# A two-layer graph transformer on one core: VectorE's order, the neighbour lists and their gathers around the first block

## The chip, the cores and the metric

The kernel runs on one NeuronCore of a Trainium2 chip. Its engines are TensorE (PE), VectorE (DVE), ScalarE (ACT), GpSimd (POOL) and SyncE (SP); each takes its instructions in the order of its own queue, and they wait for each other through semaphores. The metric is the device time of one execution in microseconds. Differences under 0.2% count as none here.

## The reference

`x` is 2708 x 512, `adj` a sparse symmetric 0/1 matrix of 2708 x 2708 with a set diagonal. Two layers of the same form are applied:

```
mask   = adj + I
q,k,v  = h @ Wq.T + bq, h @ Wk.T + bk, h @ Wv.T + bv      (8 heads of 64)
scores = q k^T / 8, and -1e9 where mask == 0
ctx    = softmax(scores) v
h1     = layer_norm(h + ctx @ Wo.T + bo)
h2     = layer_norm(h1 + relu(h1 @ W1.T + b1) @ W2.T + b2)     (2048 wide)
```

A token has few neighbours (at most 22 or so), so each row's softmax needs only those columns.

## The kernel before

**By edges.** `by_edges` makes for each token a list of its neighbours (`LIST` = 24 places) and gathers only their rows of keys and values. Tokens are ranked by the length of their list and placed anew in 22 tiles of 128, so that all tokens of a tile have nearly equal lists; `CAPS` has the length per tile. If a check on list lengths or scores fails (`flags`), a second path, `by_rows`, does the whole work densely behind a branch (`tc.If(again > 0)`).

**First pass** (`first`). For 22 tiles of tokens TensorE makes keys and values; ScalarE's queue stores them to `kv_d[0]`. Beside it the rows of `adj` are loaded, and VectorE takes each row's largest codes (`lists`). `counted` and `ranked` sort the tokens by counting; `rec` holds for each token its neighbours' numbers plus one (0: none), 32 words to a token, and goes to `rec_d`. `inverted` multiplies one-hot tables (`one`, `who`) on TensorE to get `ident_i`, the token at each new place.

**Second pass** (`first_queries`). For 22 tiles, `t` = 0 to 21, TensorE makes the queries `q` from `xT` (loads `xg` by SP), VectorE adds the bias (`qs`, L959), SP stores to `q_d`. At `t == 4` come `inverted` and the first gathers by GpSimd: 22 gathers `new<-rec_d` in all (`fetched`), some at once and later two per tile, one for each place tile. `listed` turns parts of `new` into `idx` (what the gathers of keys go by) and `minus` (what the exponential adds), at `t` = 6, 17 and 21. `new` is allotted with the tag of `hT`, the transposed input of the feed-forward, of which there is one buffer.

**Attention** (`attend`, class `Tile`). For each place tile in the order 20, 19, 18, 17, 7, 9, 6, ... the list is cut in chunks of two neighbours (the last may be one). I number the chunks: tile 20 has c1 to c3, tile 19 c4 to c6, tile 18 c7 to c10, tile 17 c11 to c14, tile 7 c15 to c19, tile 9 c20 to c24; c3, c10 and c14 have one neighbour. A chunk is: gathers `kv<-kv_d` by GpSimd, one per neighbour (five buffers, later a sixth); VectorE `kv<-kv,q` and the reduction `sc` (the scores); ScalarE `p` (exponential) and half of the weighting; VectorE `kv<-kv,p` and `acc`. A tile ends with `su`, its reciprocal, and ScalarE's division into `cx`. Gathers are asked for three chunks ahead.

**Blocks.** Two place tiles are a block: (20, 19), (18, 17), (7, 9), ... `attended` transposes `cx` (TensorE `tp`, ScalarE `cT`), multiplies by Wo (`o`) and norms (`h`, with `rd` made by GpSimd). `turned` transposes `h` into `hT`. `feed_forward` does 16 steps f: `pf` (TensorE), `ft` (ScalarE), and, three steps behind, `a`. Between the steps `advance` sends some attention for the blocks to come; at f = 10 or 11 the next block's `attended` begins.

**Who sets the order.** TensorE, ScalarE and SP follow the program's order throughout. GpSimd follows it in the first two passes and in block 0. VectorE follows it in the second pass; elsewhere a scheduler places its instructions, and it may place one of block 0 among those of the second pass.

Of the kernel before, what the change touches and what calls it, by code (L numbers as in the profile page):

```python
# [18 lines left out]
P = 128  # L19
DM = 512  # L20
# [32 lines left out]
def by_rows(ctx: ExitStack, tc: tile.TileContext, x, xT, adj, layers, out):  # L53
# [33 lines left out]
    def project(w, srcT):  # L87
# [3 lines left out]
        with tc.tile_pool(name="pw", bufs=1) as pw, tc.tile_pool(  # L91
# [20 lines left out]
            for i, (b, bw) in enumerate(blocks):  # L112
# [17 lines left out]
                for m in range(NC):  # L130
# [27 lines left out]
    def attend(kT, v):  # L158

        with tc.tile_pool(name="aq", bufs=2) as aq, tc.tile_pool(  # L160
# [130 lines left out]
            def finish(t, j, s, rb, ct):  # L291
                weigh(t, j, s, rb, ct)
                if j == NP - 1:
                    q0, r = t * P, min(P, N - t * P)
                    nc.gpsimd.dma_start(out=chunked(cT_d)[:, :, q0 : q0 + r], in_=ct[:, :, :r])

# [13 lines left out]
    def feed_forward(w, src, dst, dstT):  # L310
# [3 lines left out]
        with tc.tile_pool(name="fw", bufs=1) as fw, tc.tile_pool(  # L314
# [110 lines left out]
            def finish(i, hs, fts):  # L425
                b, bw = blocks[i]
                oT = None
                if dstT is not None:
                    oT = fx.tile([P, NC, TB], F32, tag="cg", name="oT")
                for n, t0 in enumerate(range(0, bw, P)):  # L430
                    r = min(P, bw - t0)
                    ps = ps_o.tile([P, DM], F32, tag="po", name="po")
                    for f in range(NFC):
                        nc.tensor.matmul(
                            ps[:r],
                            fts[f][:, t0 : t0 + r],
                            w2[:, f, :],
                            start=(f == 0),
                            stop=(f == NFC - 1),
                        )  # L440
# [3 lines left out]
                    nc.gpsimd.dma_start(out=dst[b + t0 : b + t0 + r, :], in_=z[:r])  # L444
                    if oT is not None:
                        flip(z, r, oT, t0)
                if oT is not None:
                    nc.gpsimd.dma_start(out=chunked(dstT)[:, :, b : b + bw], in_=oT[:, :, :bw])

# [22 lines left out]
def by_edges(ctx: ExitStack, tc: tile.TileContext, x, xT, adj, layers, out, good):  # L472
# [130 lines left out]
    def lists_of(pa):  # L603
# [21 lines left out]
        nc.gpsimd.memset(top[:, NT - 1, :], 0.0)  # L625
        rec = pa.tile([P, NT, 32], F32, tag="rec", name="rec", bufs=1)
        nc.gpsimd.memset(rec, 0.0)

# [10 lines left out]

        token = counting("token", [P, NT], [[P, NT]], 1)  # L640
        starts = counting("starts", [P, NT], [[P, NT]], 0)
# [18 lines left out]
        )  # L660
        new = dn.tile([P, NC, 2 * P], F32, tag="hT", name="new", bufs=1)
        new = new.rearrange("p c t -> p (c t)")[:, : NT * 32]
        new = new.rearrange("p (g c) -> p g c", c=32)
        nc.gpsimd.memset(new[:, NT - 1, :], 0.0)

        full = []
# [34 lines left out]
        def counted():  # L701
# [52 lines left out]
            nc.vector.tensor_scalar(flags[:, 0:1], most, 0.5, None, ALU.is_le)  # L754
            nc.vector.tensor_tensor(rec[:, :, :LIST], has, low, ALU.mult)
            return hot, before, half

        def ranked(hot, before, half):
# [39 lines left out]
            for h in range(2):  # L798
                ts = slice(h * half, (h + 1) * half)
                table = pa.tile([P, N], F32, tag=f"code{h}", name="table", bufs=1)  # L800
                wide = half * P
                one = table[:, :wide].rearrange("p (t c) -> p t c", c=P)
                who = table[:, wide : wide + half * NT].rearrange("p (t g) -> p t g", g=NT)
# [15 lines left out]
                parts.append((one, who))  # L819
            return parts  # L820

        def inverted(parts):
# [3 lines left out]
            for one, who in parts:  # L826
                for i in range(NT // 2):
                    r = size(t)
                    nc.tensor.matmul(
                        to[:, :NT],  # L830
                        one[:r, i, :],
                        who[:r, i, :],
                        start=(t == 0),
                        stop=(t == NT - 1),
                    )
                    t += 1
            nc.vector.tensor_copy(ident_i, to[:, :NT])

        def fetched(tiles):

            for g in tiles:
                r = size(g)
                gather(new[:r, g, :], rec_d, ident_i[:r, g : g + 1])

        def listed(a, b):

            some = new[:, a:b, :LIST]
            nc.vector.tensor_scalar(idx[:, a:b, :], some, 1.0, 1.0, ALU.max, ALU.subtract)
            nc.vector.tensor_scalar(minus[:, a:b, :], some, 0.0, NEG, ALU.is_equal, ALU.mult)

        return lists, counted, (ranked, inverted, fetched, listed)

# [75 lines left out]
    def first_queries(bq, wq, counts, placing, pa, tokens, meanwhile):  # L928

        nonlocal at  # L930
        ranked, inverted, fetched, listed = placing
        later = [g for g in order[4:] if 5 <= g < 12] + [g for g in order[4:] if not 5 <= g < 12]
        made = []
# [11 lines left out]
        for t in range(NT):  # L945
# [16 lines left out]
            plus_rest(qs[:r, t % 2], q, r, DK**-0.5)  # L962
            if t == OWN - 1:
                listed(NT - 5, NT - 1)
                pa.__exit__(None, None, None)
                at = ctx.enter_context(tc.tile_pool(name="at", bufs=2))
                for g in order[:3]:
                    own[g] = at.tile([P, DM], F32, tag="q", name="q", bufs=QB)
                to = dict(own)
                next(ahead)  # L970
            if t == OWN:
# [4 lines left out]
            if t == OWN + 1:  # L976
                xr = own_rows(order[3])
            if OWN < t and later:
                fetched(later[:2])
                del later[:2]  # L980
            if t == NT - 5:
                listed(5, 12)
            if t == NT - 1:
                for a, b in ((0, 5), (12, NT - 5), (NT - 1, NT)):
                    listed(a, b)
# [12 lines left out]
    def own_rows(g):  # L998
# [579 lines left out]
    def beside_queries(t):  # L1578
# [19 lines left out]

    with tc.manual_schedule(engines={mybir.EngineType.Pool}):
        made = first(layers[0], beside_keys)  # L1600
        with tc.manual_schedule(engines={mybir.EngineType.DVE}):
            first_queries(*made, beside_queries)
    behind, pool = None, []
    for n in range(NL):
# [26 lines left out]
        turning = projecting = None  # L1631
        in_order = ExitStack()
        if n == 0:
            in_order.enter_context(tc.manual_schedule(engines={mybir.EngineType.Pool}))
        for k, block in enumerate(blocks):
# [136 lines left out]
```

## Time and profile before

| | us |
|---|---|
| median of 3 runs | 1958.9 (1958.81 to 1961.58) |
| the profiled execution, whole | 1959.88 |
| its span | 1958.1 |
| TensorE busy | 1866.8 (95%) |
| VectorE busy | 1327.6 (68%) |
| ScalarE busy | 931.8 (48%) |
| GpSimd busy | 806.0 (41%) |

A line of a timeline has the start, the duration, the engine, the line of the code, the operation, what is written and read, and how often; in brackets is the engine's idle time before it and what it is taken to have waited for. A line of waits has the total, the number and the longest. "PEclk" is the granted TensorE clock in tenths.

### The profile page before, as it was taken

The page shows a single profiled execution, that of the slowest core. Times are in us where ns is not written, and L with a number is a line of the kernel's source. Part 1 is how long each engine was busy: PE and PEld are TensorE (multiplying, and loading weights), DVE is VectorE, ACT ScalarE, POOL GpSimd, SP SyncE. Part 2 cuts the span into 40 slices and gives each one's busy share as a digit, 9 for nine tenths or more (in the row PEclk, how much of TensorE's full clock was granted, in tenths as well). Part 3 has the DMA queues.
Part 4 walks back from the last instruction along what each step waited for, and adds up shares of the span by engine and source line. Part 5 has one row for each costly group of instructions (what it writes and reads, how often), then busy time and mean ns, then how long its engine had stood idle before and what let it go on. Part 6 is the DMA issues. An engine that isn't in the chain of part 4 may idle for free.

```text
span 1958.1 us, 20966 instructions
## 1 busy us (share of the span) xinstructions
PE 1866.8 (95%) x6206; PEld 1104.6 (56%) x6206; DVE 1327.6 (68%) x2188; ACT 931.8 (48%) x3219; POOL 806.0 (41%) x705
## 2 busy tenths in 40 slices
PE   9999958999999999999999997999999999999996
PEld 4444425656566566655665553566566665666663
DVE  6886665768659686685840237786977998877421
ACT  4560324645546655564451113565475767654410
POOL 2112724445536555363410124444554775545110
PEclk9999978999999999999999998999999999999998
DMA  8999837455545656454401468556665766643000
GB/s 326 356 303 321 286 112 262 167 190 194 193 144 198 212 181 209 162 184 159 148 17 65 135 242 335 179 208 205 201 220 160 255 221 220 207 155 121 17 8 11
DMA packets 133915, 366.57 MB, mean 187 GB/s; under 512 B 19290, under 2 KB 39594, under 8 KB 131084
## 3 DMA queue, kind: packets, MB, share of 16 engines
q0 software_dynamic: 68816, 245.66, 38.0%
q1 hardware_dynamic: 53332, 99.66, 14.6%
q10 hardware_dynamic: 11644, 19.83, 2.8%
q8 instruction: 50, 0.82, 0.2%
q14 instruction: 73, 0.60, 0.1%
HBM read 314.62 MB, written 50.48 MB: 186 GB/s over the span
## 4 chain that ended last, share of the span: by engine, by line
PE 40%; DVE 8%; issue 5%; DMA 3%; POOL 2%; ACT 1%; SPq 0%; POOLq 0%; DVEq 0%
PE pf L1420 16%; PE a L1393 16%; PE o L575 4%; DMA kv<-kv_d,idx 2%; DVE kv L1092 2%; DVE sc L1098 1%; PE k L575 1%; PE v L575 1%; PE tp L1228 1%; POOL kv L1055 1%; DVE acc L1131 1%; DVE kv L1124 1%; DMA q<-q_d 1%; POOL rd L1218 1%; PE q L575 1%
## 5 line engine op out<-in xcount | busy, mean ns | idle before, releaser
L1055 POOL DMA_INDIRECT kv<-kv_d,idx x420 | 548.3, 1305 | 444.1 <-DVE acc L1131 271.0
L1420 PE MATMUL pf<-hT,w 128*128 128x256 f32 (+1 forms) x2816 | 637.7, 374 | 24.0 <-ACT hT L1233 14.4
L1420 PEld LDWEIGHTS pf<-hT,w 128*128 128x128 f32 x2816 | 521.3, 191 | 198.6 <-issue 103.9
L1393 PE MATMUL a<-w,ft 128*128 128x512 f32 x1312 | 619.8, 599 | 10.4 <-ACT ft L1431 7.8
L1092 DVE TENSOR_TENSOR kv<-kv,q 128x1024 f32<-128x1024 f32 (+3 forms) x222 | 254.0, 1155 | 206.8 <-DMA kv<-kv_d,idx 175.3
L1393 PEld LDWEIGHTS a<-w,ft 128*128 128x128 f32 x1312 | 249.5, 192 | 204.8 <-issue 170.5
L1431 ACT ACTIVATE ft<-pf,b 128x256 f32<-128x256 f32 (+1 forms) x336 | 154.1, 464 | 436.9 <-PE pf L1420 436.6
L1118 ACT ACTIVATE kv<-kv,p 128x64 f32<-128x64 f32 x1232 | 311.0, 335 | 5.0
L1098 DVE TENSOR_REDUCE sc<-kv 128x16 f32<-128x1024 f32 (+3 forms) x222 | 253.7, 1151 | 1.8
L1131 DVE TENSOR_TENSOR acc<-acc,kv 128x1024 f32<-128x1024 f32 (+2 forms) x178 | 203.7, 1144 | 19.8 <-ACT kv L1118 17.3
L1218 POOL TENSOR_TENSOR rd<-va,mhalf 128x1 f32<-128x1 f32 (+1 forms) x88 | 90.2, 1025 | 293.3 <-DVE va L1216 292.3
L575 PE MATMUL o<-wo,cT 128*128 128x512 f32 x336 | 150.1, 599 | 0.5 <-ACT cT L1233 0.5
L1124 DVE TENSOR_TENSOR kv<-kv,p 128x512 f32<-128x512 f32 (+1 forms) x178 | 121.1, 681 | 38.0 <-ACT p L1111 38.0
L1162 ACT ACTIVATE cx<-acc,su 128x64 f32<-128x64 f32 (+1 forms) x352 | 88.5, 334 | 100.5 <-DVE su L1154 81.2
L1111 ACT ACTIVATE p<-sc,minus 128x8 f32<-128x8 f32 x420 | 102.7, 294 | 61.4 <-DVE sc L1098 53.9
L575 PEld LDWEIGHTS o<-wo,cT 128*128 128x128 f32 x336 | 64.2, 192 | 82.6 <-issue 72.4
L686 DVE MAX8 tops<-code 128x8 f32<-128x247 f32 (+2 forms) x242 | 83.1, 400 | 17.4 <-ACT code L683 17.4
L683 ACT ACTIVATE code<-aj 128x2708 bf16<-128x2708 int32 (+1 forms) x22 | 71.0, 3228 | 48.4 <-POOL aj L679 48.4
L1222 DVE SCALAR_TENSOR_TENSOR h<-h,rd,ln_b 128x512 f32<-128x512 f32 (+1 forms) x88 | 65.5, 745 | 41.2 <-POOL rd L1218 41.2
L1118 ACT ACTIVATE acc<-kv,p 128x64 f32<-128x64 f32 (+1 forms) x352 | 88.8, 334 | 1.4
L1480 ACT COPY kvs<-v 128x512 f32<-128x512 f32 (+1 forms) x22 | 12.9, 586 | 154.4 <-PE v L575 147.2
L1452 DVE TENSOR_TENSOR h<-a,h 128x512 f32<-128x512 f32 (+1 forms) x44 | 29.7, 675 | 82.6 <-PE a L1393 44.5
(164 smaller groups left out, 1596.9 us busy)
## 6 DMA issues: line engine op xcount, KB each, us to landing
aj<-in_adj SPq DMA_DIRECT2D x21, 1354.0 KB, 8.8
kv_d<-kvs ACTq DMA_DIRECT2D x21, 512.0 KB, 7.2
w<-in_W SPq DMA_DIRECT2D x20, 512.0 KB, 6.2
xg<-in_xT SPq DMA_DIRECT2D x19, 512.0 KB, 9.2
kv<-kv_d,idx POOLq DMA_INDIRECT x420, 5.7
w<-in_W ACTq DMA_DIRECT2D x12, 512.0 KB, 6.4
q_d<-qs SPq DMA_DIRECT2D x22, 256.0 KB, 4.7
zT_d<-zT SPq DMA_DIRECT2D x22, 256.0 KB, 4.0
```

What stands on the lines that cost most here:

```text
L575: nc.tensor.matmul(o[:r], xs(c), wm[:, c, :], start=(c == 0), stop=(c == NC - 1))
L1055: return nc.gpsimd.indirect_dma_start(out=to, out_offset=None, in_=table[:, :], in_offset=bass.IndirectOffsetOnAxis(ap=s, axis=0), bounds_ ...
L1092: nc.vector.tensor_tensor(kv[:r, :c, :DM], kv[:r, :c, :DM], self.q[:r].unsqueeze(1).to_broadcast([r, c, DM]), ALU.mult,)
L1098: nc.vector.tensor_reduce(self.sc[:r, s0 : s0 + c, :], kv[:r, :c, :DM].rearrange("p s (h d) -> p s h d", d=DK), AX.X, ALU.add,)
L1111: nc.scalar.activation(p[:r, s, :], self.sc[:r, s, :], AF.Exp, bias=minus[:r, g, s : s + 1])
L1118: nc.scalar.activation(to[:, i, hd], kv[:r, i, DM + h * DK : DM + (h + 1) * DK], AF.Copy, scale=p[:r, s0 + i, h : h + 1],)
L1124: nc.vector.tensor_tensor(to[:, 0, :].rearrange("p (h d) -> p h d", d=DK), kv[:r, 0, DM:].rearrange("p (h d) -> p h d", d=DK), p[:r, s0, : ...
L1131: nc.vector.tensor_tensor(self.acc[:r, :c, :], self.acc[:r, :c, :], kv[:r, :c, DM:], ALU.add)
L1218: nc.gpsimd.tensor_tensor(rd[:r], va[:r], mhalf[:r], ALU.pow)
L1393: nc.tensor.matmul(a[:r], fts[f][:, c0 : c0 + r], self.w2[f // 2][:, f % 2, :], start=(f == 0), stop=(f == NFC - 1),)
L1420: nc.tensor.matmul(pf[:, :w], self.w1[f // 2][:, c, f % 2 * P : f % 2 * P + P], hT[:, c, :w], start=(c == 0), stop=(c == NC - 1),)
L1431: nc.scalar.activation(ft[:, :w], pf[:, :w], AF.Relu, bias=self.b1[:, f : f + 1])
```

## The change

1. VectorE follows the program's order from the second pass on to step f = 12 of block 0, without a break; GpSimd from the start to the end of block 0, without a break.
2. `rec` is stored ready for use: 24 integers (neighbour, from 0) and 24 floats (0, or -1e9 for an empty place), 48 words to a token. `idx` and `minus` become the two halves of one tile `listed`, and a gather of `rec_d` fills both. `new`, `fetched` and the old `listed` function go. A gather `list_of(g)` comes two tiles at a time: at `t` = 4, 6 and 12 of the second pass, and at f = 0 to 7 of block 0.
3. The one-hot tables of `inverted` are bf16; the token is the sum of two products, its lane and its tile's start.
4. The attention's buffers are opened and its first gathers asked for at `t == 4` and not at 6; `attended` of block 0 comes at `t` = 17 and 18 and not at 18 and 19; tile 17's own query at `t` = 19 and not at 20; `load_next` at f = 12 and not at 10.
5. In `by_rows` four kinds of stores go by SP's queue and not by GpSimd's.

```diff
@@ by_rows (and three more stores likewise)
-                nc.gpsimd.dma_start(out=chunked(qT_d)[:, :, b : b + bw], in_=qs[:, :, :bw])
+                nc.sync.dma_start(out=chunked(qT_d)[:, :, b : b + bw], in_=qs[:, :, :bw])
...
@@ by_edges
-    idx = const.tile([P, NT, LIST], I32, name="idx")
-    minus = const.tile([P, NT, LIST], F32, name="minus")
+    listed = const.tile([P, NT, 2 * LIST], F32, name="listed")
+    idx, minus = listed.bitcast(I32)[:, :, :LIST], listed[:, :, LIST:]
+    nc.gpsimd.memset(idx[:, NT - 1, :], 0)
+    nc.gpsimd.memset(minus[:, NT - 1, :], NEG)
...
-    rec_d = dram.tile([N, 32], F32, name="rec_d")
+    rec_d = dram.tile([N, 2 * LIST], F32, name="rec_d")
...
@@ lists_of
-        new = dn.tile([P, NC, 2 * P], F32, tag="hT", name="new", bufs=1)
...
@@ counted
-            nc.vector.tensor_tensor(rec[:, :, :LIST], has, low, ALU.mult)
+            nc.vector.tensor_tensor(has, has, low, ALU.mult)
+            nc.vector.tensor_scalar(
+                rec.bitcast(I32)[:, :, :LIST], has, 1.0, 1.0, ALU.max, ALU.subtract
+            )
+            nc.vector.tensor_scalar(rec[:, :, LIST:], has, 0.0, NEG, ALU.is_equal, ALU.mult)
...
@@ ranked
+                table = table.bitcast(BF16)
...
                 nc.vector.tensor_tensor(
-                    who,
+                    match,
                     at[:, ts].unsqueeze(2).to_broadcast([P, half, NT]),
                     starts.unsqueeze(1).to_broadcast([P, half, NT]),
                     ALU.is_equal,
                 )
+                nc.vector.tensor_scalar(who[:, :, 0, :], match, lane_no, None, ALU.mult)
                 nc.vector.tensor_tensor(
-                    who, who, token[:, ts].unsqueeze(2).to_broadcast([P, half, NT]), ALU.mult
+                    who[:, :, 1, :],
+                    match,
+                    starts[:, ts].unsqueeze(2).to_broadcast([P, half, NT]),
+                    ALU.mult,
                 )
...
@@ inverted
-            nc.vector.tensor_copy(ident_i, to[:, :NT])
-
-        def fetched(tiles):
-
-            for g in tiles:
-                r = size(g)
-                gather(new[:r, g, :], rec_d, ident_i[:r, g : g + 1])
-
-        def listed(a, b):
-
-            some = new[:, a:b, :LIST]
-            nc.vector.tensor_scalar(idx[:, a:b, :], some, 1.0, 1.0, ALU.max, ALU.subtract)
-            nc.vector.tensor_scalar(minus[:, a:b, :], some, 0.0, NEG, ALU.is_equal, ALU.mult)
+            sums = pa.tile([P, 2 * NT], F32, tag="sums", name="sums", bufs=1)
+            nc.vector.tensor_copy(sums, to[:, : 2 * NT])
+            nc.vector.tensor_tensor(ident_i, sums[:, :NT], sums[:, NT:], ALU.add)
...
@@ first_queries
             if t == 4:
                 inverted(parts)
-                fetched(order[:4])
+                pa.__exit__(None, None, None)
+                at = ctx.enter_context(tc.tile_pool(name="at", bufs=2))
+                for g in order[:3]:
+                    own[g] = at.tile([P, DM], F32, tag="q", name="q", bufs=QB)
+                to = dict(own)
+                for g in order[:2]:
+                    list_of(g)
                 xrs = [own_rows(g) for g in order[:3]]
+                next(ahead)
...
+            if t in (6, 12):
+                for g in order[t // 3 : t // 3 + 2]:
+                    list_of(g)
...
-            if t == NT - 2:
+            if t == NT - 3:
...
+    def list_of(g):
+        gather(listed[: size(g), g, :], rec_d, ident_i[: size(g), g : g + 1])
...
@@ beside_queries
-        if t == NT - 4:
+        if t == NT - 5:
...
-        if t == NT - 3:
+        if t == NT - 4:
...
-    with tc.manual_schedule(engines={mybir.EngineType.Pool}):
-        made = first(layers[0], beside_keys)
-        with tc.manual_schedule(engines={mybir.EngineType.DVE}):
-            first_queries(*made, beside_queries)
+    in_order, in_turn = ExitStack(), ExitStack()
+    in_order.enter_context(tc.manual_schedule(engines={mybir.EngineType.Pool}))
+    made = first(layers[0], beside_keys)
+    in_turn.enter_context(tc.manual_schedule(engines={mybir.EngineType.DVE}))
+    first_queries(*made, beside_queries)
...
+                if f == 12:
+                    in_turn.close()
+                if k + n == 0:
+                    for g in order[6 + 2 * f : 8 + 2 * f]:
+                        list_of(g)
...
-                    if (k, f) == (0, 10):
+                    if (k, f) == (0, 12):
                         now.load_next()
```

More of the change, by code (lines that the diff above doesn't have):

```diff
@@ L294, in finish @@
                     q0, r = t * P, min(P, N - t * P)
-                    nc.gpsimd.dma_start(out=chunked(cT_d)[:, :, q0 : q0 + r], in_=ct[:, :, :r])
+                    nc.sync.dma_start(out=chunked(cT_d)[:, :, q0 : q0 + r], in_=ct[:, :, :r])
             prepare(0)
@@ L443, in finish @@
                     norm(z, r, g2, e2)
-                    nc.gpsimd.dma_start(out=dst[b + t0 : b + t0 + r, :], in_=z[:r])
+                    nc.sync.dma_start(out=dst[b + t0 : b + t0 + r, :], in_=z[:r])
                     if oT is not None:
@@ L447, in finish @@
                 if oT is not None:
-                    nc.gpsimd.dma_start(out=chunked(dstT)[:, :, b : b + bw], in_=oT[:, :, :bw])
+                    nc.sync.dma_start(out=chunked(dstT)[:, :, b : b + bw], in_=oT[:, :, :bw])
             hs = after_attention(0)
@@ L625, in lists_of @@
         nc.gpsimd.memset(top[:, NT - 1, :], 0.0)
-        rec = pa.tile([P, NT, 32], F32, tag="rec", name="rec", bufs=1)
-        nc.gpsimd.memset(rec, 0.0)
+        rec = pa.tile([P, NT, 2 * LIST], F32, tag="rec", name="rec", bufs=1)
+        lane_no = pa.tile([P, 1], F32, tag="lane_no", name="lane_no", bufs=1)
+        nc.gpsimd.iota(
+            lane_no,
+            [[1, 1]],
+            base=0,
+            channel_multiplier=1,
+            allow_small_or_imprecise_dtypes=True,
+        )
         def counting(name, shape, pattern, channel):
@@ L638, in counting @@
             return t
-        token = counting("token", [P, NT], [[P, NT]], 1)
         starts = counting("starts", [P, NT], [[P, NT]], 0)
@@ L660, in lists_of @@
         )
-        new = dn.tile([P, NC, 2 * P], F32, tag="hT", name="new", bufs=1)
-        new = new.rearrange("p c t -> p (c t)")[:, : NT * 32]
-        new = new.rearrange("p (g c) -> p g c", c=32)
-        nc.gpsimd.memset(new[:, NT - 1, :], 0.0)
         full = []
@@ L754, in counted @@
             nc.vector.tensor_scalar(flags[:, 0:1], most, 0.5, None, ALU.is_le)
-            nc.vector.tensor_tensor(rec[:, :, :LIST], has, low, ALU.mult)
+            nc.vector.tensor_tensor(has, has, low, ALU.mult)
+            nc.vector.tensor_scalar(
+                rec.bitcast(I32)[:, :, :LIST], has, 1.0, 1.0, ALU.max, ALU.subtract
+            )
+            nc.vector.tensor_scalar(rec[:, :, LIST:], has, 0.0, NEG, ALU.is_equal, ALU.mult)
             return hot, before, half
@@ L800, in ranked @@
                 table = pa.tile([P, N], F32, tag=f"code{h}", name="table", bufs=1)
-                wide = half * P
-                one = table[:, :wide].rearrange("p (t c) -> p t c", c=P)
-                who = table[:, wide : wide + half * NT].rearrange("p (t g) -> p t g", g=NT)
+                table = table.bitcast(BF16)
+                one = table[:, : half * P].rearrange("p (t c) -> p t c", c=P)
+                who = table[:, half * P : half * (P + 2 * NT)]
+                who = who.rearrange("p (t two g) -> p t two g", two=2, g=NT)
+                match = pa.tile([P, half, NT], F32, tag="match", name="match")
                 nc.vector.tensor_tensor(
-                    who,
+                    match,
                     at[:, ts].unsqueeze(2).to_broadcast([P, half, NT]),
@@ L829, in inverted @@
                     nc.tensor.matmul(
-                        to[:, :NT],
+                        to[:, : 2 * NT],
                         one[:r, i, :],
-                        who[:r, i, :],
+                        who[:r, i].rearrange("p two g -> p (two g)"),
                         start=(t == 0),
@@ L836, in inverted @@
                     t += 1
-            nc.vector.tensor_copy(ident_i, to[:, :NT])
-        def fetched(tiles):
-            for g in tiles:
-                r = size(g)
-                gather(new[:r, g, :], rec_d, ident_i[:r, g : g + 1])
-        def listed(a, b):
-            some = new[:, a:b, :LIST]
-            nc.vector.tensor_scalar(idx[:, a:b, :], some, 1.0, 1.0, ALU.max, ALU.subtract)
-            nc.vector.tensor_scalar(minus[:, a:b, :], some, 0.0, NEG, ALU.is_equal, ALU.mult)
-        return lists, counted, (ranked, inverted, fetched, listed)
+            sums = pa.tile([P, 2 * NT], F32, tag="sums", name="sums", bufs=1)
+            nc.vector.tensor_copy(sums, to[:, : 2 * NT])
+            nc.vector.tensor_tensor(ident_i, sums[:, :NT], sums[:, NT:], ALU.add)
+        return lists, counted, (ranked, inverted)
     def first(w, meanwhile):
@@ L930, in first_queries @@
         nonlocal at
-        ranked, inverted, fetched, listed = placing
-        later = [g for g in order[4:] if 5 <= g < 12] + [g for g in order[4:] if not 5 <= g < 12]
+        ranked, inverted = placing
         made = []
@@ L962, in first_queries @@
             plus_rest(qs[:r, t % 2], q, r, DK**-0.5)
[L963 to L970, printed above, removed]
+            if t in (6, 12):
+                for g in order[t // 3 : t // 3 + 2]:
+                    list_of(g)
             if t == OWN:
@@ L977, in first_queries @@
                 xr = own_rows(order[3])
[L978 to L985, printed above, removed]
             if t == OWN + 4:
@@ L1631, in by_edges @@
         turning = projecting = None
-        in_order = ExitStack()
-        if n == 0:
-            in_order.enter_context(tc.manual_schedule(engines={mybir.EngineType.Pool}))
         for k, block in enumerate(blocks):
```

## Prediction

> **What bounds the kernel now.** I read the page first, then who TensorE waited for, then the order of work on each engine around the waits. The page:
>
> ```profile
> span 1958.1 us, 20966 instructions
> PE 1866.8 (95%) x6206; PEld 1104.6 (56%) x6206; DVE 1327.6 (68%) x2188; ACT 931.8 (48%) x3219; POOL 806.0 (41%) x705
> PE   9999958999999999999999997999999999999996
> PEclk9999978999999999999999998999999999999998
> ```
>
> TensorE is busy 95% of the span, so only its holes are to be had: 1958 - 1867 = 91 us, and the largest lies in slices 6 and 7 (245 to 343 us), where the granted clock falls too. That is the passage from the first layer's projections to block 0 of its feed-forward. TensorE's waits between 180 and 420 us (total, times, longest):
>
> ```profile
> PE pf L1420 <- ACT hT L1233: 12.8, 1, 12.8
> PE pf L1420 <- ACT ft L1431: 9.7, 2, 7.3
> PE tp L1228 <- DVE qs L959: 9.4, 1, 9.4
> ```
>
> The timelines of TensorE, VectorE, ScalarE and GpSimd (start, us, what, idle before it):
>
> ```profile
> 243.13 0.60 PE L1228 MATMUL tp<-ident,cx 128*128 128x128 f32 x4
> 253.16 1.23 PE L1228 MATMUL tp<-ident,cx 128*128 128x128 f32 x4 [9.43 <-DVE qs L959]
> 254.18 5.85 PE L575 MATMUL q<-wq,xg 128*128 128x512 f32 x8
> ...
> 288.88 9.12 PE L1420 MATMUL pf<-hT,w 128*128 128x256 f32 x32 [12.77 <-ACT hT L1233]
> ...
> 328.53 3.78 PE L1420 MATMUL pf<-hT,w 128*128 128x256 f32 x8 [7.30 <-ACT ft L1431]
> ...
> 341.56 1.04 PE L1228 MATMUL tp<-ident,cx 128*128 128x128 f32 x8
> ```
> ```profile
> 234.97 0.23 DVE L1151 TENSOR_REDUCE su<-p 128x8 f32<-128x48 f32 x1
> 251.00 0.69 DVE L1092 TENSOR_TENSOR kv<-kv,q 128x512 f32<-128x512 f32 x1 [15.81 <-DMA kv<-kv_d,idx]
> 251.61 0.20 DVE L1154 RECIPROCAL su<-su 128x8 f32<-128x8 f32 x1
> ...
> 287.18 0.16 DVE L849 TENSOR_SCALAR minus<-new 128x24 f32<-128x24 f32 x1
> ```
> ```profile
> 287.42 2.18 ACT L1233 ACTIVATE hT<-tp,b 128x128 f32<-128x128 f32 x8 [19.27 <-issue]
> ```
> ```profile
> 241.51 0.96 POOL L1055 DMA_INDIRECT new<-rec_d,ident_i  x1 [0.30 <-issue]
> ...
> 245.43 1.00 POOL L1055 DMA_INDIRECT kv<-kv_d,idx  x1 [0.30 <-issue]
> ```
>
> First hole: the second `cx` needs the reciprocal at 251.61, and in VectorE's queue the score product of chunk c10 stands before it. c10's row was asked for at 245.43, because GpSimd had 22 gathers of `new` among its work, at 1.3 us each. Second hole: the page calls the 19.27 us before `hT` "issue", but `hT` and `new` share one buffer, and `hT` starts 0.1 us after the last reader of `new` ends, 11 us after the transposes (276.1). Third: `ft` stands in ScalarE's queue behind chunks whose scores wait for gathers.
>
> **What the Trainium skill says.** "TensorE: Matmul & The Clock Gate", Part 1, has the clock at half rate after about 3.4 us idle; the trace agrees (3.78 us for 8 `pf` matmuls after the 7.30 us hole, 1.89 elsewhere). The same page (architectural detail, engine queue depths) calls ScalarE's and VectorE's queues strict FIFO; 251.61 behind 251.00 is that. "VectorE: DVE Perf Modes", the perf-mode tier table, has f32 `tensor_scalar` at twice the rate of `tensor_tensor`; here 0.42 us (L707) against 0.71 (L712) for 528 elements. "SBUF — State Buffer", Who interferes with whom, says that GpSimd and a VectorE instruction with two SBUF inputs share ports; a GpSimd gather took 0.96 to 2.03 us here.
>
> **The change, part by part.**
>
> *Tables (155 to 190 us).* VectorE gains two `tensor_scalar` of 528 elements (L707's 0.42 each) and one 242-element operation per half (at most L810's 0.41): +1.6 us. The q_d store and, behind it on SP, the `xg` load for tile 6 wait for VectorE's `qs`; TensorE waited for that load until 186.28. So that point moves by 0 to +1.6; `rec_d` grows from 336 to 504 KB in a full DMA stretch, in the same bounds. I take +1. The 22 inversion products took 5.09 us in f32; in bf16 no row shows them, they take 0 to 5.09. I cost this at nothing: TensorE is then early at the same `xg`. `ident_i`: 177.2 (VectorE's idle began) + 1.6 + two operations of 0.2 = 179.2, was 179.9.
>
> *Lists.* Two list gathers and three `x` gathers come first: 179.2 + 5 x 1.3 = 185.8 for the first kv gather, was 191.74. It is covered: c1's first use waits for its query until 199. Before c10 now stand 6 list gathers, not 22: 16 x 1.3 = 21 us less of GpSimd. The conversions L848/L849 (10 instructions, about 2.5 us) go.
>
> *Program order.* TensorE runs without a hole from 187.3, and `attended` comes one tile earlier: `tp` of `cx` at 239.7 + 1 = 240.7. The reciprocal follows `su` at about 236, `cx` is ready at 238.3. First hole gone: 9.43 + 0.6 + 2.25 (slow `tp` and `q`) = 12.3 us.
>
> Then TensorE: `tp` 1.0, q18 3.45, `o` 6.9, q19, own query, q20 10.35, q21 0.9: 263.4. The second transpose of `h` needs a PSUM buffer that VectorE frees with its own-query operation: qs18 246.0, c7 and c8 scores 4.8, `kv<-kv,p` 0.7, two norms 8.8, qs19 0.6, c9 2.4, `kv<-kv,p` and `acc` 1.9, own query 0.6 = 265.8. Transpose 0.6, `hT` and its start 2.3: `pf` at **268.8**, was 288.88, 20.1 us earlier. No `listed` holds `hT`.
>
> *Block 0 up to its f = 11.* Twelve steps of 3.45 are 41.4 us (the first three are shorter). VectorE does c10 to c16 in program order, some 28 us without a pause, and ScalarE's third `ft` comes after c12 and tile 18's `cx`, which costs TensorE about 2.2 us and 1.3 of slow clock. `tp` of `cx` at 268.8 + 40 = **308.8**, was 341.56: 32.8 us earlier.
>
> *What is late next.* All 16 remaining list gathers now stand in GpSimd's queue at f = 0 to 7, two ahead of each chunk's two gathers. From c15 (about 275.8) to c22's second row stand 34 issues, 33 intervals: 14 lists, 16 of kv, 2 `q`, 2 `xb`. At 1.35 us (1.30 alone, 1.42 in the stretch 205 to 248, where VectorE works) that is 44.6 us: 320.4. A kv gather lands after 5.7 us in the median, 8 to 9 for c21 and c22 before; I take 7: 327.4. In VectorE's compiled order the scores of c20, c21 and c22 stand ahead of the norms of block 1 (both before and after). So: c22 2.4, `kv<-kv,p` and `acc` of c17 1.9, c19 2.4, `kv<-kv,p` 0.7 = 334.8, the two norms, mixed with 2.5 us of c18 and c19: 344.8. TensorE is there at 308.8 + 21.5 (as 341.56 to 363.07) = 330.3 and waits **about 12 us**, with 2 us of slow clock after. Block 1's first `pf` comes at **350.5**, was 369.10: **18.6 us earlier**.
>
> *Moved without a price.* `load_next` (three SP loads, wk on ScalarE's queue) goes from f = 10 to 12: wk is used some 50 us later. `rec`'s fill and `token` leave GpSimd where it is idle. The row-by-row path runs only if a flag fails, and the page has none of its lines: its stores cost 0. From block 1 on the order is nearly the old one, all of it shifted; I allow 3 us either way.
>
> **Sum.** Span 1958.1 - 18.6 = 1939.5; the execution had 1959.88 - 1958.1 = 1.8 around its span: 1941.3. It lay 1.0 above the median 1958.9, so **1940**.
>
> **Rivals.**
> - *The backlog is hidden* (0.20): GpSimd gets ahead while TensorE feeds, c20 to c22 land before block 1's norms. Without the 14 lists between, c22 would be issued near 304 and `pf` come near 338: 1928. For it: GpSimd idles in 249 to 268. Against: that idle is a wait for `rd` (19.66 us) that the new order keeps.
> - *One hole stays* (0.07): `cx` is late for another reason, or a slow `h` holds `hT`: 12 us less: 1948 or so, depending on the backlog.
> - *GpSimd becomes the bound* (slower 0.04, no change 0.03): the place is the same 33 intervals. Each 0.1 us on the interval costs 3.3 us, so at 1.35 + 18.6 / 33 = 1.9 us the gain is gone, and at 2.03, the longest single gather seen, it is 1962. Against: the mean stayed at 1.42 with VectorE busy.
> - That it doesn't do what it says is ruled out for the order, which is compiled; that `new` held `hT` is an inference from 0.1 us, and counts in the second rival.
>
> **Numbers.** My forecast has 0.66, with a range of its own of 1935 to 1946 (interval 1.30 to 1.42, landing 6 to 8.5 us, first point 0 to +1.6, 3 us later on). The whole range goes from the hidden backlog and 3 us, 1925, to a kept part of a hole, 1950. Faster by over 0.2% (3.9 us, about what a measurement of this kernel can tell): 0.93; within: 0.03; slower: 0.04.
>
> **What would show it.** Right: no wait of `tp` on `qs` near 243; `hT` some 1 us after its transpose; `pf` near 269; GpSimd without a pause from 276 to 320; VectorE idle 7 to 10 us each ahead of c20's and c21's scores; one hole of 10 to 13 us at the transposes of `h` near 331. Wrong: `pf` after 280, or that last hole missing, or new holes after 370.

## The result, and the profile after

The changed kernel takes **1935.41 us** (median of 4 runs, 1931.23 to 1940.67), the kernel before took 1959.96 beside it: ratio 0.9876, 95% interval 0.9849 to 0.9902. The page of the changed kernel:

```profile
span 1934.6 us, 20907 instructions
PE 1852.6 (96%) x6184; PEld 1095.7 (57%) x6184; DVE 1327.8 (69%) x2183; ACT 933.8 (48%) x3219; POOL 798.9 (41%) x705
PE   9998998799999999999999996999999999999996
PEclk9999999899999999999999998999999999999998
```

VectorE, ScalarE and GpSimd do what they did. Of the 23.5 us that the span lost, 9.3 are idle time of TensorE (91.3 before, 82.0 now) and 14.2 are busy time: 4.1 by the bf16 products of the tables (5.09, now 0.97), the rest by the same matmuls at a higher granted clock (0.977 in the mean before, 0.985 now). TensorE still bounds the kernel, and the dent of slices 6 and 7 (counted from 0) has become an 8 and a 7 in slices 7 and 8. TensorE's waits between 180 and 420 us (total, times, longest):

```profile
PE tp L1227 <- DVE h L1221: 14.7, 2, 12.0
PE q L577 <- DMA xg<-in_xT: 6.6, 1, 6.6
PE pf L1419 <- ACT ft L1430: 5.0, 3, 2.5
```

The waits for `hT` and for `qs` are gone. A wait for `h` has come: the backlog of the forecast. TensorE's timeline (start, us, what, idle before it), with the landmarks that the forecast named:

```profile
186.47 9.91 PE L577 MATMUL q<-wq,xg 128*128 128x512 f32 x16 [6.63 <-DMA xg<-in_xT]
...
242.68 1.04 PE L1227 MATMUL tp<-ident,cx 128*128 128x128 f32 x8
...
268.79 7.17 PE L1419 MATMUL pf<-hT,w 128*128 128x256 f32 x32 [0.65 <-ACT hT L1232]
...
312.52 1.04 PE L1227 MATMUL tp<-ident,cx 128*128 128x128 f32 x8
...
346.25 1.11 PE L1227 MATMUL tp<-ident,h 128*128 128x128 f32 x4 [12.05 <-DVE h L1221]
349.97 1.11 PE L1227 MATMUL tp<-ident,h 128*128 128x128 f32 x4 [2.61 <-DVE h L1221]
350.87 7.84 PE L1392 MATMUL a<-w,ft 128*128 128x512 f32 x12
358.55 7.07 PE L1419 MATMUL pf<-hT,w 128*128 128x256 f32 x32
```

What fed that hole, from the timelines of GpSimd (c15's first row and c22's second) and of VectorE (the scores of c20, c21, c22, the two norms' ends):

```profile
278.55 1.74 POOL L1054 DMA_INDIRECT kv<-kv_d,listed  x1 [2.51 <-DVE acc L1130]
...
325.48 0.99 POOL L1054 DMA_INDIRECT kv<-kv_d,listed  x1 [0.31 <-issue]
```
```profile
317.62 1.23 DVE L1091 TENSOR_TENSOR kv<-kv,q 128x1024 f32<-128x1024 f32 x1 [9.27 <-DMA kv<-kv_d,listed]
...
329.97 1.23 DVE L1091 TENSOR_TENSOR kv<-kv,q 128x1024 f32<-128x1024 f32 x1 [9.21 <-DMA kv<-kv_d,listed]
...
332.37 1.22 DVE L1091 TENSOR_TENSOR kv<-kv,q 128x1024 f32<-128x1024 f32 x1
...
345.46 0.73 DVE L1221 SCALAR_TENSOR_TENSOR h<-h,rd,ln_b 128x512 f32<-128x512 f32 x1
...
349.16 0.75 DVE L1221 SCALAR_TENSOR_TENSOR h<-h,rd,ln_b 128x512 f32<-128x512 f32 x1 [0.44 <-POOL rd L1217]
```

So far as forecast. But the span is 23.5 us shorter, and block 1's first `pf` comes only 10.55 us earlier (369.10, now 358.55). The rest, 13 us, came behind it. For that I measured each block from its first `pf` to the next block's, in all kernels of this study (us; from TensorE's timelines; the last column is the start of TensorE's last instruction):

| kernel | first `pf` of block 0 | block 0 | block 1 | block 2 | block 6 | TensorE's end |
|---|---|---|---|---|---|---|
| before | 288.9 | 80.2 | 82.2 | 82.4 | 84.1 | 1938.8 |
| own_new | 275.7 | 77.5 | 83.5 | 80.8 | 85.2 | 1924.1 |
| in_turn | 273.9 | 74.1 | 80.3 | 83.5 | 82.1 | 1917.9 |
| turn_new | 265.3 | 76.5 | 81.3 | 83.5 | 84.5 | 1910.3 |
| changed | 268.8 | 89.8 | 81.0 | 78.7 | 79.3 | 1918.0 |
| again | 266.9 | 87.3 | 82.0 | 78.9 | 78.5 | 1914.3 |
| att_back | 267.4 | 91.9 | 79.3 | 82.3 | 84.9 | 1928.8 |
| f32_hot | 267.0 | 90.6 | 83.8 | 78.3 | 78.6 | 1921.3 |
| turn14 | 267.2 | 87.4 | 81.8 | 78.4 | 78.5 | 1912.0 |
| turn_b1 | 268.2 | 74.3 | 95.8 | 78.4 | 79.2 | 1919.5 |
| lists_late | 277.8 | 69.7 | 85.3 | 78.3 | 79.0 | 1914.4 |
| late_turn14 | 274.6 | 70.7 | 82.5 | 78.9 | 78.5 | 1902.7 |
| lists_idle | 267.9 | 70.1 | 84.3 | 78.3 | 78.5 | 1901.2 |
| idle_turn14 | 269.5 | 69.7 | 83.0 | 78.6 | 78.6 | 1896.8 |

Two things stand out in it: block 0 got *longer* by the change (80.2, now 89.8), and blocks 2 and 6 got shorter by 3.7 and 4.8, which no step of the forecast has. Two changes outside the table nearly cancel: block 4 got longer by 3.0 (87.1, now 90.1), layer 1's block 1 shorter by 4.7 (76.2, now 71.5). The latter scatters: f32_hot, below, has the order of the changed kernel on every engine there, and 76.6.

### The profile page after: what moved, and what is told of

The parts are those of the page before. It is cut to its first block, busy times and chain, and to the rows that moved or that the text cites. A ratio compares the mean times of both kernels' runs of the same rounds, so it can differ in the third digit from the quotient of the medians.

```text
span 1934.6 us, 20907 instructions
## 1 busy us (share of the span) xinstructions
PE 1852.6 (96%) x6184; PEld 1095.7 (57%) x6184; DVE 1327.8 (69%) x2183; ACT 933.8 (48%) x3219; POOL 798.9 (41%) x705
## 4 chain that ended last, share of the span: by engine, by line
PE 44%; DVE 6%; issue 4%; DMA 2%; POOL 2%; ACT 2%; POOLq 0%; DVEq 0%
PE pf L1419 17%; PE a L1392 17%; PE o L577 4%; PE k L577 2%; PE v L577 2%; DVE kv L1091 1%; PE tp L1227 1%; DMA kv<-kv_d,listed 1%; DVE sc L1097 1%; POOL kv L1054 1%; DMA q_d<-qs 1%; DVE acc L1130 1%; DVE kv L1123 1%; ACT kv L1117 1%; POOL rd L1217 1%
## 5 line engine op out<-in xcount | busy, mean ns | idle before, releaser
L1054 POOL DMA_INDIRECT kv<-kv_d,listed x420 | 542.9, 1293 | 438.8 <-DVE acc L1130 252.2
L1110 ACT ACTIVATE p<-sc,listed 128x8 f32<-128x8 f32 x420 | 102.8, 294 | 91.2 <-DVE sc L1097 85.1
L577 PEld LDWEIGHTS o<-wo,cT 128*128 128x128 f32 x336 | 64.4, 193 | 82.9 <-issue 72.6
L1479 ACT COPY kvs<-v 128x512 f32<-128x512 f32 (+1 forms) x22 | 12.9, 585 | 152.8 <-PE v L577 145.5
```

The lines of the kernel that those rows point to most:

```text
L577: nc.tensor.matmul(o[:r], xs(c), wm[:, c, :], start=(c == 0), stop=(c == NC - 1))
L1054: return nc.gpsimd.indirect_dma_start(out=to, out_offset=None, in_=table[:, :], in_offset=bass.IndirectOffsetOnAxis(ap=s, axis=0), bounds_ ...
L1110: nc.scalar.activation(p[:r, s, :], self.sc[:r, s, :], AF.Exp, bias=minus[:r, g, s : s + 1])
```

## The experiments

Ratios are to runs of the kernel before on the same chip, with 95% intervals. Between two kernels of this table some 4 us can be told apart.

| kernel | median us | ratio |
|---|---|---|
| again | 1934.65 | 0.9861 (0.9840 to 0.9882) |
| own_new | 1944.85 | 0.9915 (0.9894 to 0.9936) |
| in_turn | 1935.33 | 0.9861 (0.9840 to 0.9882) |
| turn_new | 1931.45 | 0.9843 (0.9820 to 0.9865) |
| lists_late | 1930.06 | 0.9830 (0.9816 to 0.9845) |
| turn14 | 1936.76 | 0.9885 (0.9869 to 0.9902) |
| late_turn14 | 1926.95 | 0.9827 (0.9809 to 0.9845) |
| f32_hot | 1938.40 | 0.9867 (0.9847 to 0.9886) |
| att_back | 1946.67 | 0.9910 (0.9890 to 0.9930) |
| lists_idle | 1919.41 | 0.9780 (0.9761 to 0.9800) |
| idle_turn14 | 1914.35 | 0.9752 (0.9735 to 0.9769) |
| turn_b1 | 1934.84 | 0.9846 (0.9820 to 0.9872) |

**again: does a second execution show the same waits?** (This is the control in what follows.)

> The changed kernel once more, unedited. Its first trace gained 10.6 us up to block 1's first pf (369.10 before, 358.55 after) and 13 us more behind that point, where the order of work is nearly the old one, in waits of 1 to 4 us at the head of blocks. Theory (the later waits belong to the kernel's order): block 1's first pf at 358 to 360 again, the end of the last pf group again 20 to 21 us ahead of before, time 1933 to 1938. Rival (the later waits scatter from one execution to the next): some of the waits in blocks 2 to 8 come out different by 2 to 4 us each, and the last pf moves against the first trace by 3 us or more.

Block 1's first `pf` came at 354.2, 4 us earlier than expected, and the end moved with it by 3.7, which the rival had set as its sign. But the lead was there before the blocks that were in doubt: blocks 2 and 6 repeat within 0.8 us. Their gains belong to the kernel and not to one execution.

**own_new: the shared buffer alone.** The kernel before, with

```diff
-        new = dn.tile([P, NC, 2 * P], F32, tag="hT", name="new", bufs=1)
+                new = wts.tile([P, NC, DM], F32, tag="wk", name="new")   # allotted at the first gather
```

> The kernel before, with new in a buffer of its own (that of wk, free by then) instead of hT's. Theory (new held hT): hT follows its transposes by 1 to 3 us, the 12.8 us wait of pf on hT falls to 2.3, block 0's first pf comes 10 us earlier (about 279, was 288.88), and part of that is given back at the third ft, whose chunks wait for gathers: 1949 to 1957. Rival (ScalarE's order or a late chunk held hT): the wait stays over 10 us, 1960.

TensorE's waits around the two holes:

```profile
252.82 1.23 PE L1231 MATMUL tp<-ident,cx 128*128 128x128 f32 x4 [8.07 <-DVE qs L962]
275.68 5.45 PE L1423 MATMUL pf<-hT,w 128*128 128x256 f32 x24 [0.72 <-ACT hT L1236]
```

The wait for `hT` fell from 12.77 to 0.72, the first hole stayed (8.07): `new` did hold `hT`. It is worth 17 us in the medians (1961.76 for the kernel before in this comparison), more than the 5 to 13 expected.

**in_turn: VectorE's order alone.** The kernel before, with

```diff
+    in_turn.enter_context(tc.manual_schedule(engines={mybir.EngineType.DVE}))
     first_queries(*made, beside_queries)
...
+                if f == 12:
+                    in_turn.close()
```

> The kernel before, with VectorE in program order up to f = 12 of block 0 as in the changed kernel, nothing else. Theory (the order cures the reciprocal's wait, but new still holds hT until the last gather of new has landed and been read near 287): the 9.4 us wait of tp on qs shrinks or goes, the wait for hT grows by as much, block 0's first pf stays at 285 to 290, time 1952 to 1962. Rival (the order alone makes the gain): first pf near 277, 1945 or less. Rival on the other side (program order puts the layer's queries behind c10's late gather): the waits of TensorE on VectorE between 243 and 290 grow, 1965.

(GpSimd's two regions become one as well, but its order is the same up to 357 us.) The time is that of the whole change. VectorE's, GpSimd's, ScalarE's and TensorE's timelines:

```profile
236.10 0.20 DVE L1154 RECIPROCAL su<-su 128x8 f32<-128x8 f32 x1
...
272.23 0.16 DVE L849 TENSOR_SCALAR minus<-new 128x24 f32<-128x24 f32 x1
```
```profile
242.37 0.96 POOL L1055 DMA_INDIRECT new<-rec_d,ident_i  x1 [0.30 <-DMA new<-rec_d,ident_i]
...
246.28 1.00 POOL L1055 DMA_INDIRECT kv<-kv_d,idx  x1 [0.30 <-issue]
```
```profile
272.47 2.18 ACT L1233 ACTIVATE hT<-tp,b 128x128 f32<-128x128 f32 x8 [15.89 <-issue]
```
```profile
243.99 1.04 PE L1228 MATMUL tp<-ident,cx 128*128 128x128 f32 x8
...
273.93 6.43 PE L1420 MATMUL pf<-hT,w 128*128 128x256 f32 x19 [9.39 <-ACT hT L1233]
```

Two readings follow. First, the 22 list gathers still stand ahead of c10, whose row is asked for at 246.28, later than before (245.43); and yet the first hole is gone, since the reciprocal no longer stands behind c10's product. The gathers were not the cause; the place in VectorE's queue was. Second, `hT` still starts 0.1 us after the last reader of `new` ends, but that reader has come from 287.18 to 272.23. I had taken 287 for the landing of the gathers; the last was asked for at 242.37. What made it late is VectorE's queue again: the 14.95 us gained are close to the 15.81 us that VectorE stood idle ahead of c10's product in the kernel before, and all behind it was late with it. So the order gains at both holes: the time is near the first rival's, while the wait for `hT` stays, as my theory had it.

**turn_new: both.**

> The kernel before, with both: VectorE in program order up to f = 12 and new in its own buffer; the lists are still gathered in one go ahead of c10 and converted afterwards. Theory (both holes are needed to go, and the 22 list gathers ahead of c10 are the third part): second hole gone, a first hole of 5 to 12 us stays since the queries stand behind c10, whose row is asked for near 245; behind that no backlog in block 0: 1940 to 1950. Rival (order and buffer are the whole change): block 0's first pf at 267 to 271 as in the changed kernel, 1930 to 1938.

First `pf` of block 0, and the `hT` ahead of it:

```profile
265.27 5.02 PE L1423 MATMUL pf<-hT,w 128*128 128x256 f32 x22 [0.72 <-ACT hT L1236]
```
```profile
263.82 2.18 ACT L1236 ACTIVATE hT<-tp,b 128x128 f32<-128x128 f32 x8 [7.22 <-PE tp L1231]
```

The rival has it: neither hole is left, with all the lists gathered in the old way. Nothing of the new lists, their earlier gathers or the bf16 tables is needed for block 0's start, which is 1.6 to 3.5 us earlier here than in the two executions of the changed kernel.

**lists_late: the lists out of block 0.** The changed kernel, with

```diff
-                if k + n == 0:
-                    for g in order[6 + 2 * f : 8 + 2 * f]:
-                        list_of(g)
...
+            if n == 0 and s0 == 0 and order.index(g) >= 5:      # in loads()
+                for nx in order[order.index(g) + 1 :][:1]:
+                    list_of(nx)
```

> The changed kernel, with the list of each tile from the seventh on asked for when the tile ahead of it begins its gathers, instead of two at each f = 0 to 7 of block 0: 13 of the 14 list gathers between c15 and c22 go. Theory (GpSimd's backlog of issues makes the 12.05 us wait for h): c22's second issue at 278.6 + 20 x 1.42 = 307 instead of 325.5, the wait of the transposes of h goes or falls under 3 us, block 1's first pf at 340 to 345 (358.55), and 1917 to 1924 if the blocks behind keep it. Rival (the gathers wait for free kv buffers or for their landing, not for their turn): c22's issue stays at 320 or later, the wait stays over 9 us, 1933 to 1938.

TensorE's timeline, the new wait and the transposes of `h`:

```profile
227.90 4.64 PE L577 MATMUL q<-wq,xg 128*128 128x512 f32 x5 [7.33 <-DVE qs L968]
...
341.44 1.04 PE L1230 MATMUL tp<-ident,h 128*128 128x128 f32 x8
```

The wait for `h` is gone: block 0 takes 69.7 us, not 87 to 90. But most of the lists now stand outside the part where GpSimd keeps the program's order, and the scheduler set 12 of them ahead of c6's rows (issued from 202.6 to 219.3); there TensorE has a new wait of 7.33 us. VectorE's `qs`, for which it waited, itself waited 6.89 us for something that the trace does not name, so the link to the lists is only by place. The backlog was moved, not removed, and the time is 6 us above the expected range.

**turn14: the norms ahead of the late scores.** `if f == 12` becomes `if f == 14` in the changed kernel.

> The changed kernel, with VectorE kept in program order up to f = 14 instead of f = 12, so that c21's and c22's scores stand behind block 1's norms; GpSimd's order and its 14 lists are as they were. Theory (the wait for h is VectorE's place in the queue behind late gathers): c22's issue stays near 325, but the norms no longer wait for it, the wait for h falls from 12.05 to under 3 us, block 1's first pf at 340 to 346, 1917 to 1925. Rival (program order brings the same late chunks ahead of something else): a wait of 5 us or more on an ft, on cx or on h in block 1, 1928 to 1940.

The transposes of `h` on TensorE:

```profile
342.54 1.12 PE L1227 MATMUL tp<-ident,h 128*128 128x128 f32 x4 [8.65 <-DVE h L1221]
346.96 1.12 PE L1227 MATMUL tp<-ident,h 128*128 128x128 f32 x4 [3.30 <-DVE h L1221]
```

The edit did not do what I meant: in the compiled order only c20's score went behind the norms. c21's and c22's come later in the program than the region's end, and the scheduler still hoisted them into it. As a test of the theory it says nothing; the wait stayed.

**late_turn14: the last two together.**

> Both of the last two edits. Theory (both remove one and the same hole): no more than the better of the two alone, within 3 us, 1915 to 1924. Rival (they remove different holes): better than either by over 6 us.

1926.95, 3 us from lists_late alone, with overlapping intervals: within the 3 us expected, but above the range of time, since a wait of 6.54 us like that of lists_late is in it too. That both edits remove one and the same hole isn't shown by this, as turn14 alone removed none.

**turn_b1: the norms first, the backlog kept.** VectorE's region is closed at f = 12 of block 1, GpSimd's at the end of block 1.

> The changed kernel, with both program-order regions (VectorE's and GpSimd's) kept open to block 1 (VectorE's to its f = 12, GpSimd's to its end). turn14 had not moved what it meant to: c21's and c22's scores were still hoisted ahead of block 1's norms. Here c20, c21 and c22 all stand behind them, and GpSimd's 14 lists between c15 and c22 stay. Theory (the wait for h is VectorE's queue standing behind late gathers): c22's second issue stays at 320 to 326, the wait of the transposes of h (11.2 and 2.6 us in the control) falls to under 3 us in all, block 1's first pf at 336 to 343. Rival (the norms themselves, or the xb rows behind the backlog, are late): the wait stays over 8 us, block 1's first pf at 350 or later. For the time: 1915 to 1930 if block 1 in program order is no worse, more if it is.

GpSimd's timeline (c22's second row) and TensorE's waits:

```profile
324.81 0.99 POOL L1054 DMA_INDIRECT kv<-kv_d,listed  x1 [0.31 <-issue]
```
```profile
336.23 0.66 PE L1227 MATMUL tp<-ident,h 128*128 128x128 f32 x4 [2.61 <-DVE h L1221]
342.54 7.17 PE L1419 MATMUL pf<-hT,w 128*128 128x256 f32 x32 [0.50 <-ACT hT L1232]
356.46 2.08 PE L564 MATMUL pr<-dg,ones 128*128 128x128 f32 x8 [5.04 <-DVE dg L558]
...
424.82 3.78 PE L1419 MATMUL pf<-hT,w 128*128 128x256 f32 x8 [4.34 <-ACT ft L1430]
```

The theory holds at its place: the backlog is as long as ever, and the hole is gone, block 1's first `pf` at 342.5. It takes both to make the hole, the late gathers and the norms behind them in one queue. Block 1 in program order then cost 95.8 us in place of 81 to 82 and gave it all back. Two waits make 9.4 of that: for `dg`, which VectorE has at 318.8 in the changed kernel and here behind block 0's last norms and a chunk, at 356.1; and for an `ft` that stood in ScalarE's queue behind the exponential of a chunk whose score was late.

**f32_hot: the tables in float32.** The line `table = table.bitcast(BF16)` goes.

> The changed kernel with its one-hot tables in float32. Theory (the 22 products are covered by the wait for xg): they take 5.1 us instead of 0.97, the 6.63 us wait for xg shrinks by the difference, the queries resume at 186 to 187 as before, and the 16 matmuls behind them run in 7.1 instead of 9.9 us since the clock is not lowered by a long wait: 1932 to 1936, no loss. Rival (the inversion is on the path of the first gathers): ident_i 3 to 5 us later, c1 to c3 later by as much, 1938 to 1941.

TensorE behind the wait for `xg`:

```profile
187.46 7.13 PE L577 MATMUL q<-wq,xg 128*128 128x512 f32 x16 [2.69 <-DMA xg<-in_xT]
```

The 22 products take 5.12 us here, 0.97 in bf16; the wait for `xg` takes the difference, and the 16 matmuls behind it run in 7.13 and not 9.91. Block 0's first `pf` is at 267.0, as in the control (266.9). The median lies 2 us above the expected range, where the rival would have it, with an interval that overlaps the control's; the rival's mechanism is not there, for the first list gather is asked for 1.0 to 1.3 us later (180.23), not 3 to 5. But the load of `xg` landed 2.6 us later than in the control (187.46, 184.89), and the first `pf` did not: the 16 matmuls, at full clock, made it up. bf16 gains nothing that I can measure.

**att_back: `attended` one tile later again.**

```diff
-        if t == NT - 5:
+        if t == NT - 4:
             through(0)
...
-        if t == NT - 4:
+        if t == NT - 3:
             for _ in blocks[0]:
```

(tile 17's own query goes back to `t` = 20 with it.)

> The changed kernel, with block 0's attended (and the last own query) put back one tile of queries later, where the kernel before has it. What is at stake: in the six kernels built on the changed one block 2 of layer 0 (first pf to first pf of block 3) takes 78.3 to 78.9 us and block 6 78.5 to 79.3, in the four built on the kernel before 80.9 to 83.5 and 82.1 to 85.2; that is most of the 13 us found behind block 1. Theory (attended a tile earlier shifts how many chunks each later step takes, and with it VectorE's order in all later blocks): block 2 at 80.5 to 84, block 6 at 81.5 to 85, the wait for h near 343 still there, time 1940 to 1947. Rival (the lists' form, or the place from which they are gathered, shortens those blocks): blocks 2 and 6 stay under 79.5, time 1933 to 1940.

Blocks 2 and 6 take 82.3 and 84.9 again, the time is 12 us longer, and two waits of the kernel before are back, for `ft` in block 2 and for `h` in block 6:

```profile
514.84 5.40 PE L1392 MATMUL a<-w,ft 128*128 128x512 f32 x8 [2.03 <-ACT ft L1430]
...
844.26 1.11 PE L1227 MATMUL tp<-ident,h 128*128 128x128 f32 x4 [4.44 <-DVE h L1221]
```

In the compiled order the instructions of VectorE and GpSimd from block 1's norms to the end of layer 1 stand as in in_turn, operation by operation. So the theory holds for these blocks: a tile's shift at the start sets VectorE's order in blocks hundreds of microseconds away. (`attended` and tile 17's own query were moved together, and not tried apart.) Not all of the 12 us is order: blocks 2 and 6 are 3.4 and 6.4 us longer than in the control, and another 6.2 lie in layer 1's block 1, where the order is the same and the time scatters.

**lists_idle: the lists where GpSimd was idle.** No lists in block 0, but

```diff
             if t == OWN + 1:
                 xr = own_rows(order[3])
+            if t == OWN + 2:
+                for g in order[6:14]:
+                    list_of(g)
...
         if t == NT - 4:
+            for g in order[14:]:
+                list_of(g)
             for _ in blocks[0]:
```

> The changed kernel, with its last 16 list gathers in program order at two places where GpSimd stood idle: 8 behind the row gather of the fourth tile (it idled from 201.3 to 212.5) and 8 ahead of block 0's norms (239.6 to 255.8). lists_late took the wait for h away, but its lists were hoisted in front of c5 and c6 and cost 7.3 us at 228. Theory (the backlog can be paid for where GpSimd is idle): no wait at 228 over 2 us, block 0's first pf at 266 to 270, no wait for h over 3 us before block 1, whose first pf comes at 337 to 342, blocks 2 and 6 as short as in the changed kernel: 1917 to 1924. Rival (the chunks behind are then held by free kv buffers or VectorE instead): a wait of 5 us or more elsewhere in block 0, first pf of block 1 at 347 or later, 1926 to 1932.

TensorE's waits between 180 and 420 us, then c22's second row on GpSimd and block 1's first `pf`:

```profile
PE q L577 <- DMA xg<-in_xT: 6.0, 1, 6.0
PE pf L1422 <- ACT ft L1433: 2.3, 2, 1.9
PE tp L1230 <- DVE h L1224: 2.3, 1, 2.3
PE tp L1230 <- DVE q L1015: 1.6, 1, 1.6
```
```profile
307.55 1.45 POOL L1057 DMA_INDIRECT kv<-kv_d,listed  x1 [0.30 <-DMA xb<-in_x,ident_i]
```
```profile
337.95 7.07 PE L1422 MATMUL pf<-hT,w 128*128 128x256 f32 x32
```

All as expected: block 1's first `pf` at 337.95, no hole, 1919.41. c22's row is asked for at 307.55 (325.48 in the changed kernel). Where the change puts its lists costs it 15 us (1934.65 in the control).

**idle_turn14: the same with `f == 14`.**

> The same with VectorE in program order up to f = 14. With the lists out of the way, theory (nothing late is left ahead of block 1's norms, so their place no longer matters): within 3 us of lists_idle. Rival (VectorE's order decides by itself): 4 us or more faster than lists_idle.

1914.35, the fastest of all: 0.9752 of the kernel before, and faster than the changed one as well. It is 5 us ahead of lists_idle, so the rival's number came; but its mechanism isn't shown. Block 1's first `pf` is no earlier (339.2, 337.9), and the 4.4 us by which TensorE ends earlier lie in blocks 1 and 4 and in layer 1's block 1. VectorE's order differs from that of lists_idle between 275 and 362 us alone, so in block 4 and in layer 1 it is the same. What makes this kernel faster stays open.

## Why the prediction was right, and where not

The time forecast was 1940, it is 1935.4: the sign and the range held. That it came so near is luck: 8 us lost up to block 1 and 12.9 gained behind it nearly cancel. Its terms, in us gained (the first two counted from the start, the next two added to them):

| term | forecast | measured |
|---|---|---|
| up to block 0's first `pf` | 20.1 | 20.1 |
| up to block 1's first `pf` | 18.6 | 10.55 |
| block 1 to TensorE's end | 0, within 3 | 10.2 |
| behind it | 0 | 2.7 |
| whole span | 18.6 | 23.5 |

- *Tables.* Forecast: the queries behind `xg` 1 us later, the bf16 products at no cost. The queries resumed 0.2 us later (186.47, was 186.28), but their 16 matmuls took 9.91 us and not 7.13, and the transposes of `xr` behind them came 3.0 us later (196.22, was 193.25). The bf16 products are done sooner and so lengthen the wait for `xg` (6.63, 2.69 in f32_hot, 1.16 before), and the granted clock behind it was 0.50 (187 to 190 us). In the nine traces with bf16 tables these 16 matmuls took 8.64 to 10.13 us; in f32_hot 7.13, at a granted clock of 1.00. Its transposes come no earlier than the control's (194.43, 194.29) only because its load landed later. In seven traces (changed, again, f32_hot, turn14, turn_b1, lists_idle, idle_turn14) block 0's first `pf` comes 72.6 us behind these transposes, so the loss is not made up before it. "Costs nothing" was wrong by 1.5 to 3.0 us at this place; no median shows it.
- *First hole.* Gone, `tp` of `cx` at 242.68 (forecast 240.7). The reason given was in part wrong: the 21 us taken from GpSimd were not needed (in_turn).
- *Second hole.* Gone, `pf` at 268.79 (forecast 268.8). The agreement to the hundredth is luck: `tp` of `cx` came 2.0 us late, and the way from there to `pf`, 28.1 us in the forecast, took 26.1. That `new` held `hT` is shown (own_new, turn_new). Beside the new order, a buffer of its own for `new` brings the first `pf` 8.7 us forward in the traces (273.93, 265.27), but only 3.9 us of median between in_turn and turn_new, about what can be told apart.
- *Backlog.* The mechanism is shown by two experiments from two sides: lists_idle takes the gathers away, turn_b1 the place in the queue. The forecast lost 8.0 us in its terms: c15's issue 2.8 late, the interval 1.42 (46.9 us by 33) and not the 1.35 that I took, 2.4 more; the landing was 6.9 (7 taken) and the way from there to the norms' end 17.5 (17.4). The last 2.9 came behind the wait: 12 matmuls `a` took 7.84 us, not 5.32. I had named 2 us of slow clock and left them out of the sum for `pf`. The wait itself, 12.05, is the 12 that I forecast, with both of its ends late: TensorE came to it at 334.2 and not at 330.3, since it took 43.7 us and not 40 from block 0's first `pf` to the transposes of the next `cx`.
- *The rival "the backlog is hidden"* did not occur, but its price was near: c22 at 304 and `pf` at 338 without the lists; lists_idle has 307.55 and 337.9. Of the other rivals, no old hole stayed, and GpSimd's interval was 1.42. The 2.03 us that I took there for the longest gather is that of the trace up to 420 us; the longest of the whole trace before took 3.61.
- *"From block 1 on the order is nearly the old one, all of it shifted"* is the step that failed. I allowed 3 us behind block 1's first `pf`, and 10.2 came. Blocks 2 and 6 give 8.5 of that, and att_back shows the cause for them; the 4.7 us of layer 1's block 1 scatter, and block 4 takes 3.0 back. I had looked at that order and taken a few exchanged instructions, scores and sums of chunks between 409 and 824 us of the kernel before, for harmless; the waits that went with them are those for `ft` in block 2 and for `h` in block 6.
- *"Stores cost 0".* The four kernels built on the one before need 15.1 to 15.3 us from the start of the last store of `out` to the span's end, the changed one and the nine built on it 12.2 to 12.8. The two last stores, on GpSimd (spans 1958.1 and 1934.6):

```profile
1942.86 1.03 POOL L1018 DMA_INDIRECT out<-h,ident_i  x1 [1.08 <-DVE h L1222]
```
```profile
1922.07 1.04 POOL L1017 DMA_INDIRECT out<-h,ident_i  x1 [1.09 <-DVE h L1221]
```

  Behind it stands only the branch around `by_rows`, where the change moves four kinds of stores off GpSimd's queue. That these make the 2.7 us is argued from the place; no run took them back alone.

The parts fit together. turn_new has the order and the buffer (1931.45); `attended` a tile earlier is worth 12.0 (att_back against again); together 1919.4, and lists_idle, which has these and no lists in block 0, measures 1919.41. That this agrees to the hundredth is chance: each median is good to some 4 us, and no run shows that the 12.0 are the same without the lists in block 0. The lists at f = 0 to 7 then cost 15.2 and give the control's 1934.65. The new form of the lists and the bf16 tables gain nothing that shows.

## What to carry to other kernels

Ask of each late result what stands ahead of it in its engine's queue before asking what is slow: the first hole here and the new one were short operations behind a product that waited for a gather, and the second hole came late by the same product, since the last reader of `new` stood behind it too. Work that is moved must go to a place where its engine is idle, read from the timeline; the same 16 gathers cost 15 us in block 0 and nothing that shows in two gaps of 11 and 16 us. And where each step takes as much of the work ahead as a running credit allows, as `advance` does here, a shift at the start can change the order of stages far behind it, so that order is to be compared instruction by instruction.

## What was not expected of the hardware

After the 12.05 us wait the granted clock was 0.50 in the whole stretch from 346 to 355 us, and 1.00 from 356. "TensorE: Matmul & The Clock Gate" of the Trainium skill (Part 1, the table of the two states) has full speed again after some 3.4 us of sustained work. Here the 12 matmuls of 7.84 us, of 0.43 at full and 0.86 at half speed, mean about 6 slow ones: an estimate of 5 us from 350.87, between one and two of the page's windows, which it says run freely, so the two do not disagree. The four transposes at 346.25, with 2.61 us of waiting behind them, did not bring the clock back.
